# Twenty seeded key shifts after the rounds of a list scheduler, in a two-layer conditioned attention kernel

## The chip, the core and the metric

The kernel runs on one core of one Trainium2 chip. The metric is device microseconds of one execution, taken as the median over runs. The core has a matrix engine (TensorE; PE in the profile, and PEld for its weight loads), three others that compute (VectorE, DVE; ScalarE, ACT; GpSimd, POOL), and SyncE (SP), which here issues nearly all DMAs. Each engine executes its own list of instructions in the order in which the program gives them, and waits on semaphores for the others.

## The reference

Eight sequences of 512 tokens and 512 features pass through two layers, each of which adds its result to its input; all is float32.

```python
# layer 0: linear attention, 8 heads of 64
xn = ln(x)
q = softmax over the head's features of (xn @ Wq + bq)
k = softmax over the tokens of (xn @ Wk + bk + (1 - mask) * -1e6)
v = (xn @ Wv + bv) * mask
y = q @ (k^T v)                       # per head
h = ln(y) * (1 + scale) + shift       # scale, shift = split(silu(emb) @ W_emb + b_emb)
x = x + silu(h) @ W_out + b_out
# layer 1: softmax attention, 16 heads of 32
att = softmax over m of (q_n . k_m + (1 - mask_m) * -1e6)
y = att @ v ; the rest as in layer 0
```

## The kernel before

The kernel writes no engine's list by hand. It records every operation into an object `Order`, then `Order.place` computes a start time and an engine for each operation, and `Order.issue` (the helper on line 483, which is why nearly every row of the profile says L483) emits them sorted by start time. So the order on every engine comes from this planner, which runs on the host before the launch and costs no device time.

**The work.** Layer 0 goes batch by batch: load x, normalise, transpose it on TensorE, project with split weights (a high and a low part of each operand, three products of four matmuls of 512 columns each), softmax, attention, hidden layer, output. Layer 1 works on groups G of four heads (32 groups, four for each batch): `l1_qk` projects, and writes high and low parts `hl` to DRAM (`dWk<-hl`, `dWq<-hl`); `l1_stack` reads them back stacked (`kst<-dWk`, `qst<-dWq`); `l1_max` computes all scores once (`mm<-qst,kst` with 98 rows), takes the row maxima on DVE (`nm<-mm`), transposes them (`mi`), copies them out on ACT (`z<-mm`), and sends them by DMA into rows 98 to 106 of the stack (`qst<-z`); `l1_att` computes the scores a second time with 106 rows, so that the maximum is already subtracted, and ACT takes the exponential (`A<-mm`); `l1_av` multiplies by v in four column groups of 32 (`mm<-A,v`, eight instructions a block) and `A<-A,A` on POOL or DVE sums the exponentials. The last group is done by `l1_last` in halves, and after it come the hidden layer and output of the last batch.

**The planner.** An operation (`Op`) has the engines that may run it with a duration for each (`_takes`), its dependences (`deps`, `soft`), and the tiles that it opens (`fresh`), each of which waits for a free buffer. `pack` is a list scheduler: it keeps a clock for every engine, takes the engine that can start something earliest, and gives it, of the operations that are ready at that time, the one with the smallest `key`; an engine is not kept idle for a more urgent operation that is not ready yet. `slack` then walks backwards from the end and sets each key to the latest start that the operations behind it allow. The first keys are the program's order. A round is one `pack` and one `slack`; `place` does twelve and keeps the placement that ends first. Besides the durations the planner charges TensorE for three things:

```python
if at > now[e] + 1.0:
    o.start += WEIGHTS                      # 110 ns after any wait
elif many != narrow:
    o.start += ENTER if many else LEAVE     # 95, 150 ns around a block in column groups
```

A DMA ends 2400 ns (`DMA_LAND`) after its bytes have passed one common pipe of 260 bytes a ns, and its issue takes 560 ns of its queue.

Of 'A<-A,A' and of a few other operations the planner also chooses the engine (`order.on("gpsimd", "vector")`).

Of the kernel before, what the change touches and what calls it, by code (L numbers as in the profile page):

```python
# [172 lines left out]
class Op:  # L173
    __slots__ = (
        "seq", "engines", "calls", "takes", "late", "deps", "users", "waits", "tiles", "fresh",
        "ready", "start", "end", "engine", "bytes", "key", "soft", "after",
    )


ENTER, LEAVE = 95.0, 150.0  # L180
ROUNDS = 12
LINK = {"PE": 55.0, "ACT": 36.0, "DVE": 36.0, "POOL": 90.0, "SP": 60.0}
WEIGHTS = 110.0
DMA_ISSUE, DMA_LAND, DMA_RATE = 560.0, 2400.0, 260.0
# [2 lines left out]
class Room:  # L187
# [6 lines left out]
    def lets(self, place, taken):  # L194
        free = len(self.free) - taken
        if place == self.head + taken:
            return free > 0
        return self.loose and free > 1

    def take(self, place):  # L200
        self.gone.add(place)
        while self.head in self.gone:
            self.gone.discard(self.head)
            self.head += 1
        return heapq.heappop(self.free)
# [8 lines left out]
class Order:  # L214
# [44 lines left out]
    def add(self, name, calls, takes, late, nbytes=0):  # L259
        if not isinstance(takes, dict):  # L260
            takes = {name: takes}
        o = Op()
        o.seq, o.calls, o.late, o.bytes = len(self.ops), calls, late, nbytes
        o.takes = {ENGINES[k]: (k, v) for k, v in takes.items()}
        o.deps, o.soft, o.users, o.after, o.tiles, o.fresh = set(), set(), [], [], [], []
        o.start = o.end = o.engine = None
        o.key = o.seq
        for t in self.hold:
            self.touch(o, t, None, True)
        self.hold = []  # L270
        for method, args, kw in calls:
            outs, ins = [args[0]], list(args[1:])
            for k, v in kw.items():
                (outs if k == "accum_out" else ins).append(v)
            for v in ins:
                if isinstance(v, View):
                    self.touch(o, v.tile, v.box(), False)
            for v in outs:
                if isinstance(v, View):
                    box = v.box()  # L280
                    if method == "matmul":
                        box = (*box[:2], 0, 511)
                    self.touch(o, v.tile, box, True)
        o.deps.update(self.behind)
        o.soft -= o.deps | {o}
        for d in o.deps:
            d.users.append(o)
        for d in o.soft:
            d.after.append(o)
        self.ops.append(o)  # L290

# [23 lines left out]
        kept.append((o, box, write))  # L315
        t.seen = kept

    def place(self, rounds=ROUNDS):

        best = None  # L320
        for _ in range(rounds):
            end = self.pack()
            if best is None or end < best[0]:
                best = end, [(o.start, o.end, o.engine, [t.slot for t in o.fresh]) for o in self.ops]
            self.slack(end)
        for o, (o.start, o.end, o.engine, slots) in zip(self.ops, best[1]):
            for t, t.slot in zip(o.fresh, slots):
                pass
        return best[0]

    def slack(self, end):

# [1137 lines left out]
```

## Time and profile before

| | |
|---|---|
| median of 3 runs | 1383.26 us (1383.21 to 1383.97) |
| the profiled execution, its own time | 1382.37 us |
| its span, first to last instruction | 1380.3 us |
| instructions | 20884 |
| mean granted TensorE clock | 0.993 |
| DMA | 158.85 MB, mean 115 GB/s |

The profile is of one execution, so a sum made from it stands against 1382.37 us, of which 2.1 us lie outside the span; the median lies 0.9 us above. Layer 0 fills the span to about 527 us, layer 1 the rest. In the views, a time is in microseconds from the start of the span; a busy time of an engine is the union of its instructions, and the matmul's end is modelled, so that PE's busy time includes what lies between the starts of two matmuls as long as the first one's end is later than the second one's start.

### The profile page before, as it was taken

How to read it: one execution, taken by the hardware profiler on the slowest of the kernel's cores; microseconds unless marked ns; L12 is line 12 of the kernel's file. 1: busy time of each engine (PE TensorE's matmuls, PEld its weight loads, DVE VectorE, ACT ScalarE, POOL GpSimd, SP SyncE). 2: the span in 40 equal slices, each digit the busy share in tenths (PEclk: the TensorE clock that was granted, in tenths of full speed). 3: DMA queues.
4: the chain of work that ended last, by engine and by line, in shares of the span. 5: the costliest groups of instructions: out<-in, count | busy, mean ns of one | idle time of the engine just before them, and what ended most of it. 6: DMA issues, size and time to landing. Idle time of an engine off the chain costs nothing.

```text
span 1380.3 us, 20884 instructions
## 1 busy us (share of the span) xinstructions
PE 1345.3 (97%) x7363; PEld 944.0 (68%) x7363; DVE 1034.7 (75%) x1771; ACT 747.8 (54%) x1400; POOL 684.2 (50%) x748
## 2 busy tenths in 40 slices
PE   6999999999999999999999999999999999999987
PEld 4788788888888886566566566566666566666645
DVE  6676576666767777887878787778878867878966
ACT  4433334433345535556847756855855864764773
POOL 6222504133232525676555647548538636655663
PEclk9999999999999999999999999999999999999999
DMA  6332203012221374553263364463563544445312
GB/s 226 132 129 93 98 5 100 32 69 92 69 100 60 112 236 114 142 150 110 94 178 98 94 186 106 116 185 69 153 173 76 151 140 110 140 119 140 95 43 69
DMA packets 77375, 158.85 MB, mean 115 GB/s; under 512 B 8556, under 2 KB 8680, under 8 KB 77248
## 3 DMA queue, kind: packets, MB, share of 16 engines
q1 hardware_dynamic: 77152, 157.41, 38.9%
q8 instruction: 58, 0.95, 0.3%
q14 instruction: 45, 0.37, 0.1%
q0 software_dynamic: 64, 0.08, 0.0%
q10 hardware_dynamic: 56, 0.04, 0.0%
HBM read 104.92 MB, written 50.48 MB: 113 GB/s over the span
## 4 chain that ended last, share of the span: by engine, by line
PE 90%; ACT 3%; DMA 3%; DVE 2%; issue 1%; POOL 1%; SPq 0%; ACTq 0%; POOLq 0%
PE mm L483 90%; DMA qst<-z 2%; ACT mm L483 1%; DMA qst<-dWq 1%; ACT y L483 1%; DVE nm L483 0%; DMA v<-x 0%; DVE xc L483 0%; DMA dWq<-hl 0%; ACT xT L483 0%; DVE A L483 0%; ACT z L483 0%; ACT A L483 0%; DMA v<-in_mask_BxS_ff 0%; DVE xT L483 0%
## 5 line engine op out<-in xcount | busy, mean ns | idle before, releaser
L483 POOL TENSOR_TENSOR A<-A,A 128x512 f32<-128x512 f32 x249 | 332.7, 1358 | 214.1 <-PE mm L483 148.2
L483 DVE TENSOR_REDUCE nm<-mm 128x1 f32<-128x512 f32 x512 | 332.7, 683 | 71.4 <-PE mm L483 68.3
L483 ACT ACTIVATE A<-mm 128x512 f32<-128x512 f32 x450 | 251.1, 602 | 144.3 <-PE mm L483 136.8
L483 PE MATMUL mm<-kst,qst 98*128 98x512 f32 x512 | 202.6, 422 | 4.5 <-DMA qst<-dWq 2.3
L483 PE MATMUL mm<-qst,kst 106*128 106x512 f32 (+1 forms) x528 | 194.6, 409 | 3.6 <-DMA qst<-z 3.4
L483 PEld LDWEIGHTS mm<-kst,qst 98*128 98x128 f32 x512 | 97.0, 192 | 73.0 <-issue 21.4
L483 PE MATMUL mm<-A,v 128*32 128x512 f32 (+1 forms) x932 | 145.4, 593 | 0.0
L483 PEld LDWEIGHTS mm<-qst,kst 106*128 106x128 f32 x528 | 98.7, 192 | 55.8 <-issue 15.8
L483 POOL TENSOR_TENSOR y<-y,bo 128x512 f32<-128x512 f32 x60 | 78.1, 1308 | 101.2 <-DMA y<-in_x 90.8
L483 PE MATMUL mm<-Wvh,xT 128*128 128x512 f32 x384 | 120.2, 402 | 0.0
L483 PE MATMUL mm<-xT,Wkh 128*128 128x512 f32 x384 | 117.4, 413 | 1.2 <-ACT xT L483 0.8
L483 ACT ACTIVATE mm<-mm,cols 128x512 f32<-128x512 f32 x64 | 48.2, 753 | 121.9 <-PE mm L483 121.9
L483 PE MATMUL mm<-ident,xc 128*128 128x128 f32 x512 | 92.5, 284 | 14.9 <-DVE xc L483 12.0
L483 POOL TENSOR_SCALAR v<-bWv,cols 128x512 f32<-128x512 f32 x64 | 48.2, 768 | 115.2 <-PE mm L483 115.2
L483 ACT ACTIVATE y<-mm,shL,scL 128x128 f32<-128x128 f32 (+1 forms) x144 | 76.4, 531 | 51.0 <-PE mm L483 48.5
L483 PEld LDWEIGHTS mm<-ident,xc 128*128 128x128 f32 x512 | 65.1, 144 | 44.4 <-DVE xc L483 13.6
L483 DVE TENSOR_TENSOR A<-A,A 128x512 f32<-128x512 f32 x73 | 83.6, 1155 | 14.9 <-PE mm L483 12.3
L483 PEld LDWEIGHTS mm<-xT,Wkh 128*128 128x128 f32 x384 | 69.8, 191 | 22.3 <-ACT xT L483 6.0
L483 PEld LDWEIGHTS mm<-Wvh,xT 128*128 128x128 f32 x384 | 71.7, 189 | 16.5 <-issue 1.7
L483 ACT ACTIVATE mm<-mm,shL,scL 128x128 f32<-128x128 f32 (+2 forms) x152 | 76.1, 501 | 7.2 <-PE mm L483 7.2
L483 PE MATMUL mm<-xT,Wqh 128*128 128x512 f32 x256 | 76.4, 399 | 0.3 <-DVE nm L483 0.2
L483 POOL MEMSET bWk<- 64x4 f32 (+1 forms) x24 | 5.9, 245 | 136.1 <-PE mm L483 135.4
(204 smaller groups left out, 2704.1 us busy)
## 6 DMA issues: line engine op xcount, KB each, us to landing
kst<-dWk SPq DMA_DIRECT2D x96, 256.0 KB
qst<-dWq SPq DMA_DIRECT2D x96, 256.0 KB
dWk<-hl SPq DMA_DIRECT2D x32, 512.0 KB
dWq<-hl SPq DMA_DIRECT2D x32, 512.0 KB
xc<-in_x SPq DMA_DIRECT2D x32, 256.0 KB
y<-in_x SPq DMA_DIRECT2D x32, 256.0 KB
x<-y SPq DMA_DIRECT2D x32, 256.0 KB
xc<-x SPq DMA_DIRECT2D x32, 256.0 KB
```

What stands on the lines that cost most here:

```text
L483: getattr(engine, method)(*args, **kw)
```

## The change

The planner does eight rounds in place of twelve, and goes on from the keys after the best of them. Twenty times, `moved` draws from a fixed seed a share (1, 3 or 10 per cent) of the operations' groups and a spread (500, 2000 or 6000 ns), and shifts the keys of each drawn group by a Gaussian number; a group is the operations whose first tile has the same name without digits, within 120 operations of the program's order. Two rounds follow from the shifted keys, and the result replaces the best only if it ends earlier by the planner's own clock. At the end the best keys are packed once more. The lists of users, which were filled in the order of a Python set, are now filled in the program's order. No recorded operation, duration, buffer count or constant of the planner's charges is changed.

```diff
+import random
@@ class Op
-        "ready", "start", "end", "engine", "bytes", "key", "soft", "after",
+        "ready", "start", "end", "engine", "bytes", "key", "soft", "after", "group",
-ROUNDS = 12
+ROUNDS = 8
+MOVES = (30003, 30024, 30032, 30040, 30090, 30221, 30224, 30234, 30236, 30247, 30369, 30408, 30455, 30462, 30463, 30480, 30512, 30517, 30536, 30622)
@@ def add
-        for d in o.deps:
+        for d in sorted(o.deps, key=lambda d: d.seq):
             d.users.append(o)
-        for d in o.soft:
+        for d in sorted(o.soft, key=lambda d: d.seq):
             d.after.append(o)
@@
-    def place(self, rounds=ROUNDS):
-
-        best = None
-        for _ in range(rounds):
+    def place(self):
+
+
+        best = self.rounds([o.seq for o in self.ops], ROUNDS)
+        for seed in MOVES:
+            best = min(best, self.rounds(self.moved(best[1], seed), 2), key=lambda r: r[0])
+        self.rounds(best[2], 1)
+        return best[0]
+
+    def rounds(self, line, n):
+        best = (1e12,)
+        for o, key in zip(self.ops, line):
+            o.key = key
+        for _ in range(n):
+            line = [o.key for o in self.ops]
             end = self.pack()
-            if best is None or end < best[0]:
-                best = end, [(o.start, o.end, o.engine, [t.slot for t in o.fresh]) for o in self.ops]
             self.slack(end)
-        for o, (o.start, o.end, o.engine, slots) in zip(self.ops, best[1]):
-            for t, t.slot in zip(o.fresh, slots):
-                pass
-        return best[0]
+            if end < best[0]:
+                best = end, [o.key for o in self.ops], line
+        return best
+
+    def moved(self, line, seed):
+        draw = random.Random(seed)
+        share, size = draw.choice([0.01, 0.03, 0.1]), draw.choice([500.0, 2000.0, 6000.0])
+        shift = {g: draw.gauss(0.0, size) for g in self.groups() if draw.random() < share}
+        return [key + shift.get(o.group, 0.0) for o, key in zip(self.ops, line)]
+
+    def groups(self):
+        for o in self.ops:
+            o.group = re.sub(r"\d", "", o.tiles[0].name), o.seq // 120
+        return sorted({o.group for o in self.ops})
```

## The prediction

> **What bounds the kernel now.** I read the page first, for which engine fills the span:
>
> ```profile
> span 1380.3 us, 20884 instructions
> PE 1345.3 (97%) x7363; PEld 944.0 (68%) x7363; DVE 1034.7 (75%) x1771; ACT 747.8 (54%) x1400; POOL 684.2 (50%) x748
> PE 90%; ACT 3%; DMA 3%; DVE 2%; issue 1%; POOL 1%; SPq 0%; ACTq 0%; POOLq 0%
> ```
>
> TensorE is busy for 1345.3 of 1380.3 us and carries 90% of the chain that ended last. The next engine, DVE, has 345 us to spare. The change adds and removes no matmul, so order can only win back what TensorE loses: 35.0 us of idle time, stretches at a lower clock, and small gaps that the busy time conceals. The busy time by stages tells where the idle part lies (columns: stretch and its length, busy time with instructions of PE, PEld, DVE, ACT, POOL, then granted clock, DMA share, GB/s):
>
> ```profile
> 0.00:18.30 18.30, 4.90 (x18) 3.21 (x18) 10.03 (x19) 5.66 (x9) 11.51 (x30) 1.00 0.84 271
> 18.30:527.00 508.70, 508.34 (x3075) 417.57 (x3076) 351.07 (x699) 207.31 (x368) 167.67 (x258) 1.00 0.29 97
> 527.00:533.00 6.00, 4.06 (x29) 3.32 (x28) 3.75 (x8) 5.91 (x11) 5.38 (x5) 1.00 0.79 222
> 533.00:541.00 8.00, 8.00 (x25) 4.29 (x24) 7.17 (x12) 4.91 (x9) 0.34 (x2) 0.57 0.94 224
> 570.00:1297.00 727.00, 721.43 (x3679) 457.23 (x3678) 577.46 (x917) 456.84 (x873) 434.14 (x399) 1.00 0.46 127
> 1297.00:1377.00 80.00, 70.12 (x397) 41.36 (x395) 59.09 (x86) 50.24 (x104) 42.28 (x39) 0.91 0.27 75
> ```
>
> Idle: 13.4 us in the head, 0.4 in layer 0, 1.9 at the border of the layers, 0.5 between 541 and 570, 5.6 in layer 1, 9.9 in the tail, and 3.3 after TensorE's last matmul. The fourth row's clock of 0.57 over 8 us is 3.4 us lost; the tail's 0.91 over 70 busy us is 6.3 us.
>
> The timeline of PE in layer 1 shows the concealed gaps (start, length, instruction):
>
> ```profile
> 614.96 0.40 PE L483 MATMUL mm<-kst,qst 98*128 98x512 f32 x1
> 615.19 0.39 PE L483 MATMUL mm<-Wvl,xT 128*128 128x512 f32 x1
> 615.51 1.06 PE L483 MATMUL mm<-A,eg 128*32 128x512 f32 x8
> 616.39 1.04 PE L483 MATMUL mm<-A,v 128*32 128x512 f32 x8
> 617.37 0.73 PE L483 MATMUL mm<-Wvl,xT 128*128 128x512 f32 x2
> ...
> 619.93 0.48 PE L483 MATMUL mm<-Wvh,xT 128*128 128x512 f32 x1
> 620.25 0.39 PE L483 MATMUL mm<-kst,qst 98*128 98x512 f32 x1
> ```
>
> Matmuls of 512 columns start 0.23 to 0.24 us apart. Into the block in column groups it takes 0.32, so 0.09 more. Two blocks behind one another are 0.88 apart, and out of the second it takes 0.98, so 0.10 more: a block that stands alone costs 0.19 us beyond its work. From 619.93 to 620.25 a lone step takes 0.32, again 0.09 more: a weight load that came late because it waited. None of this is idle time. The planner charges 95, 150 and 110 ns for these three, so it sees what the chip pays, a little dear. Its durations also stand near the rows: by its formula 685 ns for `nm<-mm` (the groups show 683), 598 for `A<-mm` on ACT (602), 1408 for `A<-A,A` on POOL (1358). I take from this that most of an earlier end by its clock should be an earlier end on the chip.
>
> **The change, by stages.** By its own clock the search can't end later than its first eight rounds; the first eight may end later than the best of twelve, and what the shifts find is not in any row. So I bound each stage by what TensorE loses there and by what the rule of `pack` lets a key change.
>
> *Head* (13.4 us idle). The chain shows DVE's `xc` waiting for POOL's `rsf`, which stands behind the mask's work. But the `mvf` that POOL's next step needs is done at 7.1 us, POOL's `hl` from 6.81 to 8.07 was already running, and `pack` never holds an engine idle. What a key can change is `mbd<-hl` (8.37 to 8.95) ahead of `vef` (9.03): 0 to 0.7 us. I take 0.5.
>
> *Layer 0* (0.4 us idle in 508.7): TensorE is full. I take 0, with 2 us either way for the small gaps.
>
> *Border of the layers.* TensorE idles 1.94 us before 532.80, waiting for the last parts of `xT`. The chain there is ACT's:
>
> ```profile
> 527.91 0.62 ACT Woh L483
> 528.52 0.66 ACT mm L483
> ...
> 529.69 0.57 ACT z L483
> ```
>
> `Woh` is the cast of a weight whose partner is finished at 533 us and later; with another key it stands behind `mm`, and 0.62 us, with `z` 1.2 us, leave the chain. If the gap goes, the 3.4 us at the lower clock behind it may go too: 0 to 5.3 us. I take the middle, 2.7. What is late next is DMA `qst<-z`, issued at 530.28, whose reader starts at 534.80, behind a wait of 0.64 us of the weight load.
>
> [...]
>
> *Layer 1, 570 to 1297.* Idle 5.6 us. The waits of weight loads, from 600 to 1297 (us in total, times, longest):
>
> ```profile
> PEld mm L483 <- issue: 78.9, 175, 0.8
> PEld mm L483 <- ACT A L483: 29.6, 63, 0.9
> ```
>
> With the smaller rows of the same answer these are some 360 waits; at 0.09 us, 32 us. The blocks are 31 groups of heads by four, 124; at 0.19, 24 us. Together with the idle time 61 us are at stake, but each block stands where its exponentials are ready, and the rate is even (509 matmuls from 600 to 700, 508 from 800 to 900), so I count on one part in fifteen: 4 us. Bounds: 12 us gained (a fifth), 6 lost (a tenth, if the shifted order meets more waits than the planner believes).
>
> *Tail* (1297 to the end, 83.3 us). Idle 9.9 and 6.3 at the lower clock. The chain:
>
> ```profile
> 1305.31 8.34 DMA qst<-dWq
> 1329.19 3.09 DMA qst<-z
> 1349.64 4.61 DMA v<-x
> ```
>
> The three reads `qst<-dWq` are issued behind three `kst<-dWk`, `kst<-mbd` and a `y<-x` on SP; the `v<-x` delays only POOL's `v` ahead of `veb` and `rsb`. Both are matters of order, and here a few places decide the end directly. Bounds: 15 us gained, 3 lost. I take a third, 5. The last 3.3 us, one DVE addition and its store, stay.
>
> Sum: 0.5 + 0 + 2.7 + 4 + 5 = 12.2 us. 1382.4 - 12.2 = 1370.2 for the profiled execution; the median lies 0.9 higher, 1371.
>
> **The rivals.**
>
> *The maxima's round trip falls due (slower).* In each of 32 groups, `nm`, `mi`, `z` and the DMA `qst<-z` must be through before `mm<-qst,kst`. The trace shows the DMA at 3.1 to 4.2 us in the chain, TensorE idle for it 3.4 us in six places and weight loads 1.8 in five. The planner prices it at 3.5 us from issue and knows no contention; shifts that pull the second scores up to that price make the shortfall of 0.7 (4.2 - 3.5) due at all 32: 22 us against 12 gained, 1393. It decides once more than half of the groups wait. Against it: twenty shifts that touch at most a tenth of the groups hardly reach all 32. Chance 0.11.
>
> *The chip does not follow, or the shifts find little (no change).* If eight rounds end about as late as twelve and few shifts lower the end, or what they save is lost to waits that the planner misses: within 2.8 us of 1383.3. For it: TensorE is full in 92% of the span. Chance 0.10.
>
> *The gain is near the bounds.* Border 5, layer 1 10, tail 10, head 0.7: 26 us, 1357. For it: the clock returns with the gaps, which the planner doesn't even count. Against it: it needs three stages at once. Chance 0.14.
>
> **How the numbers follow.** The forecast, 1371 with 1361 to 1380 of its own, has 0.65. Faster by over 0.2% (2.8 us, about what a measurement of this kernel can tell from no change) is 0.65 + 0.14 = 0.79, no change 0.10, slower 0.11. The range leaves out most of the slower rival and the lower half of the large gain: 1357 to 1384.
>
> **What the profile would show.** The same 7363 matmuls, PE busy near 1339 us and idle time near 29 (about half of the 12 us is idle time, by the shares above). Right: a tail from the last `dWq<-hl` on shorter by some 5 us, with PE's clock above 0.91; no stretch at 0.57 behind the border, or a shorter one; fewer than 360 waits of weight loads in layer 1. The split of `A<-A,A` between POOL and DVE may shift without meaning. Wrong: PE idle before `mm<-qst,kst` on `qst<-z` above 15 us (the slower rival); or the stages as long as before to 1 us each (the second); or a gain that lies in layer 0, which I hold to be full.

## The result and the profile after

The changed kernel takes 1387.89 us (median of 7 runs, 1386.20 to 1393.48) against 1383.21 us before (7 runs): ratio 1.0041, 95% interval 1.0026 to 1.0055. It is slower by 0.4%, where 1371 us was forecast. The profiled execution has a span of 1384.4 us, 4.1 us more than before.

The page of the changed kernel:

```profile
span 1384.4 us, 20891 instructions
...
PE 1343.9 (97%) x7363; PEld 940.1 (68%) x7363; DVE 1043.3 (75%) x1776; ACT 746.6 (54%) x1400; POOL 681.0 (49%) x743
...
PE 91%; DVE 4%; ACT 2%; DMA 2%; issue 1%; POOL 0%; SPq 0%; ACTq 0%; DVEq 0%
```

The work is the same: 7363 matmuls, and five sums have gone from POOL to DVE (1771 to 1776, 748 to 743). But TensorE is idle for 40.5 us instead of 35.0, and DVE's part of the chain has doubled to 4%. The busy time by the stages of the prediction:

```profile
18.30:527.00 508.70, 508.70 (x3072) 415.91 (x3073) 350.05 (x699) 207.26 (x369) 165.30 (x257) 1.00 0.29 97
527.00:533.00 6.00, 5.58 (x35) 4.15 (x34) 5.72 (x9) 5.63 (x10) 4.94 (x5) 1.00 0.93 232
533.00:541.00 8.00, 8.00 (x39) 5.50 (x38) 7.16 (x12) 5.47 (x10) 1.59 (x3) 1.00 0.92 237
541.00:570.00 29.00, 27.57 (x137) 15.52 (x135) 25.29 (x37) 16.62 (x31) 22.74 (x17) 0.94 0.38 109
570.00:1297.00 727.00, 715.10 (x3640) 450.86 (x3640) 579.66 (x909) 451.30 (x859) 427.06 (x391) 1.00 0.45 126
```

At the border the gap of 1.94 us and the stretch at a lower clock are gone (from 533 to 541 the clock is 1.00 with 39 matmuls, where it was 0.57 with 25), though a smaller gap has opened behind them (28.5 to 27.6 busy us, clock 0.94). Layer 1 has lost: 715.1 busy us and 3640 matmuls in the same 727 us, against 721.4 and 3679. Most of it lies in one place. The same 40 us of both kernels, the kernel before first, the changed one second:

```profile
1140.00:1180.00 40.00, 40.00 (x218) 25.22 (x218) 32.90 (x56) 20.80 (x41) 30.27 (x29) 1.00 0.37 90
```

```profile
1140.00:1180.00 40.00, 36.51 (x189) 23.02 (x188) 32.62 (x50) 16.41 (x30) 23.13 (x21) 0.96 0.39 100
```

Twenty-nine matmuls fewer. The timeline of the changed kernel there (start, length, instruction, and in brackets the idle time before it and what ended it):

```profile
1152.04 1.29 POOL L504 TENSOR_TENSOR A<-A,A 128x512 f32<-128x512 f32 x1
...
1153.28 1.29 POOL L504 TENSOR_TENSOR A<-A,bWq 128x512 f32<-128x512 f32 x1
1153.50 6.01 DVE L504 CAST mi<-nm 128x16 fp32r<-128x16 f32 x1
...
1154.52 2.52 POOL L504 TENSOR_TENSOR A<-A,A 128x512 f32<-128x512 f32 x2
...
1157.00 1.27 POOL L504 TENSOR_TENSOR A<-A,bWk 128x512 f32<-128x512 f32 x1
...
1158.22 1.27 POOL L504 TENSOR_TENSOR A<-A,A 128x512 f32<-128x512 f32 x1
...
1159.55 0.17 DVE L504 TENSOR_TENSOR mi<-nm,mi 128x16 fp32r<-128x16 f32 x1
...
1159.87 1.01 PE L504 MATMUL mm<-ident,mi 128*8 128x128 f32 x4 [3.49 <-DVE mi L504]
```

A cast of 16 elements a partition, which elsewhere lasts as little as 0.17 us, lasts 6.01 us. It ends as POOL's run of sums ends (1158.22 + 1.27 = 1159.49, against 1153.50 + 6.01 = 1159.51); each of the sums starts before the one ahead of it has ended. The profile counts the cast as busy time of DVE, so it is part of DVE's total (1034.7 us before, 1043.3 now) and of no wait. TensorE runs out of work and idles 3.49 us, and from 1159.4 its clock is 0.51 for 3.4 us.

**Where the plan and the chip part.** `place` gives each instruction of TensorE a planned start, and the trace holds the same instructions in the same order, so the two can be laid side by side. The table takes the transposes of the maxima (`mm<-ident,mi`) of some of the 32 groups as marks. Columns two and three are the kernel before; the others are differences from it, of the planned start (P) and of the start in the trace (T).

| mark | before P | before T | change P | change T | change, DVE relieved T |
|---|---|---|---|---|---|
| group 0 (layer 0 ends) | 524.6 | 529.0 | -3.0 | 0.0 | +0.6 |
| group 1 (border) | 545.5 | 550.3 | -3.6 | -1.1 | -0.8 |
| group 23 | 1118.2 | 1127.3 | -6.8 | +2.3 | -0.8 |
| group 25 | 1168.7 | 1178.7 | -6.8 | +7.4 | -0.7 |
| group 30 (tail begins) | 1288.1 | 1298.1 | -8.2 | +6.5 | -1.6 |
| end | 1367.1 | 1380.3 | -8.5 | +4.1 | -4.1 |

By its own clock the change ends 8.5 us earlier. On the chip it is level through layer 0, gains 1.1 us at the border, loses 3.4 up to group 23 and 5.1 from there to group 25, and takes back 0.9 up to group 30 and 2.4 in the tail. The last column is an experiment below, with the same planned starts.

Each T column is one execution. What happens between groups 23 and 25 repeats in the runs below: the three traces of the changed order with the stall (`pair_after`, the changed kernel again, and `after_mi` among them) take 56.4 to 56.5 us from mark to mark, the two with DVE relieved 51.4 and 51.5, and the five with the order before 51.4 to 51.5. The ends repeat less well. A second trace of the kernel before (`pair_before`) ends 5.1 us after the first, and a second trace with DVE relieved (`pair_after_lopool`) ends 1.1 us ahead of it, not 4.1.

Eight rounds in place of twelve, and the ordered lists, do nothing: without any shift the new planner gives every operation the planned start and engine that it has in the kernel before. The twenty shifts are the whole change.

### The profile page after: what moved, and what is told of

The parts are those of the page before. It is cut to its first block, busy times and chain, and to the rows that moved or that the text cites. A ratio compares the mean times of both kernels' runs of the same rounds, so it can differ in the third digit from the quotient of the medians.

```text
span 1384.4 us, 20891 instructions
## 1 busy us (share of the span) xinstructions
PE 1343.9 (97%) x7363; PEld 940.1 (68%) x7363; DVE 1043.3 (75%) x1776; ACT 746.6 (54%) x1400; POOL 681.0 (49%) x743
## 4 chain that ended last, share of the span: by engine, by line
PE 91%; DVE 4%; ACT 2%; DMA 2%; issue 1%; POOL 0%; SPq 0%; ACTq 0%; DVEq 0%
PE mm L504 91%; DVE nm L504 1%; ACT mm L504 1%; DVE A L504 1%; DVE mi L504 1%; ACT y L504 1%; DMA qst<-z 1%; DVE xc L504 0%; POOL A L504 0%; DMA rawL0Wk<-in_L_cond_Wk 0%; DMA out<-y 0%; DVE y L504 0%; DMA v<-in_mask_BxS_ff 0%; ACT A L504 0%; DVE stf L504 0%
## 5 line engine op out<-in xcount | busy, mean ns | idle before, releaser
L504 POOL TENSOR_TENSOR A<-A,A 128x512 f32<-128x512 f32 x243 | 329.2, 1376 | 212.4 <-PE mm L504 126.2
L504 PE MATMUL mm<-A,v 128*32 128x512 f32 (+1 forms) x932 | 141.7, 586 | 0.3 <-ACT A L504 0.2
L504 PE MATMUL mm<-Wvh,xT 128*128 128x512 f32 x384 | 125.2, 407 | 0.0
L504 PE MATMUL mm<-xT,Wkh 128*128 128x512 f32 x384 | 121.1, 415 | 1.9 <-ACT xT L504 1.4
L504 PE MATMUL mm<-ident,xc 128*128 128x128 f32 x512 | 101.6, 286 | 16.6 <-DVE xc L504 12.5
L504 DVE TENSOR_TENSOR A<-A,A 128x512 f32<-128x512 f32 x79 | 89.1, 1135 | 14.9 <-PE mm L504 10.4
L504 ACT ACTIVATE hl<-mm,cols 128x512 fp32r<-128x512 f32 x64 | 44.2, 691 | 54.5 <-PE mm L504 47.8
```

What stands on the lines that cost most here:

```text
L504: getattr(engine, method)(*args, **kw)
```

## The experiments

Medians of the kernel before differ from set to set (1381.5, 1390.3, 1382.6 and 1384.2 us in the four sets below, the last two on one chip), so kernels are compared within a set; a ratio is to the kernel before in the same set.

**First set: the cast, and part of the shifts.** `after_mi` and `before_mi` issue the cast as a reduction; the plan stays the same to the nanosecond.

```diff
-        nc.vector.tensor_copy(mi[:, :, 0, :], nm)
+        nc.vector.tensor_reduce(mi[:, :, 0, :], nm.unsqueeze(3), AX.X, ALU.max)
```

> The changed kernel with the same placement; only the first of the two small instructions on the maxima (the cast mi<-nm, 128x16, SBUF to SBUF, on DVE) is issued as a reduction over an axis of length one, with the same result. Theory 'held cast': in the trace of the changed kernel one cast lasts 6.01 us, as long as POOL runs sums back to back, and TensorE then idles 3.5 us and has half the clock for 3.4 us; if a reduction is not held, this costs nothing, and the kernel falls by about 5 us to 1382 to 1384, no cast above 0.3 us. Rival 'spread loss': the search's gains are lost in many small pieces, and the one stall only stands for time that would be lost elsewhere: 1386 to 1389.

Measured: 1386.5 us, ratio 1.0028 (1.0005 to 1.0051). The reduction is not held (0.15 to 0.17 us in all 32 groups), but the next DVE instruction is, at the same place and to the end of the same run of sums (1152.96 + 5.86 = 1158.82, against 1157.53 + 1.26 = 1158.79; timeline of `after_mi`):

```profile
1152.58 1.28 POOL L504 TENSOR_TENSOR A<-A,bWq 128x512 f32<-128x512 f32 x1
1152.75 0.17 DVE L504 TENSOR_REDUCE mi<-nm 128x16 fp32r<-128x16 f32 x1
...
1152.96 5.86 DVE L504 TENSOR_TENSOR mi<-nm,mi 128x16 fp32r<-128x16 f32 x1
...
1153.83 2.52 POOL L504 TENSOR_TENSOR A<-A,A 128x512 f32<-128x512 f32 x2
...
1156.31 1.25 POOL L504 TENSOR_TENSOR A<-A,bWk 128x512 f32<-128x512 f32 x1
...
1157.53 1.26 POOL L504 TENSOR_TENSOR A<-A,A 128x512 f32<-128x512 f32 x1
...
1158.96 0.60 PE L504 MATMUL mm<-ident,mi 128*8 128x128 f32 x4 [3.34 <-DVE mi L504]
```

So the experiment did not take the stall away (TensorE still idles 3.34 us) and decided nothing on its cost. It shows what is held: not every DVE instruction at this point, for the reduction ran through while POOL was busy, though its operands lie in SBUF as well; held were the cast and the subtraction.

> The kernel before, placement unchanged, with the same replacement of the cast by a reduction. 'Held cast': its casts last 0.56 us in the median and 2.4 at most, nearly all hidden behind TensorE's other work, so 0 to 2 us faster (1381 to 1383). 'Spread loss': the same as before, 1383. If it falls by 5 us or more, the cast's delay is a cost of both kernels alike and no reason for their difference.

Measured: 1380.3 us, ratio 0.9997 (0.9972 to 1.0023): no change, as both theories had it.

The first five and the first ten shifts alone:

```diff
-MOVES = (30003, ..., 30622)
+MOVES = (30003, 30024, 30032, 30040, 30090)
```

> The changed planner with the first five of the twenty shifts: by the planner's clock 3.0 us earlier than the kernel before. 'Held cast': 1380 to 1383, as long as no cast above 3 us appears in its trace. 'Spread loss': within 1 us of 1383 or above it, with the lateness against the planner's clock 3 us larger than before's.

> The first ten of the twenty shifts: by the planner's clock 5.7 us earlier than the kernel before. 'Held cast': 1378 to 1382 unless a cast above 3 us appears. 'Spread loss': 1383 to 1387, rising with the number of shifts.

Measured: 1387.6 us (1.0028, 1.0004 to 1.0052) and 1385.6 us (1.0029, 1.0002 to 1.0056). Neither has a cast above 1.31 us, so "held cast", which had both at 1383 us or below, fails on both. The timeline of `moves5` has another DVE instruction held, a sum, behind three of POOL's and into the instructions that follow:

```profile
607.26 3.78 POOL L504 TENSOR_TENSOR A<-A,A 128x512 f32<-128x512 f32 x3
...
607.55 4.04 DVE L504 TENSOR_TENSOR A<-A,bWq 128x512 f32<-128x512 f32 x1
```

That explains at most 3.4 us of it (4.04 less the 0.68 of the shortest sum `A<-A,A` of this shape on DVE in the trace of before). The time does not rise with the number of shifts either, against "spread loss"; the planned gain of 3.0 and 5.7 us simply does not appear.

**Second set: DVE relieved, and controls without a gain.** In `after_lopool` and `before_lopool` the subtraction is issued on POOL as well, at its place in the planned order; planned starts are unchanged.

```diff
+                    if method == "tensor_tensor" and o.tiles[-1].tag == "mi":
+                        nc.gpsimd.tensor_tensor(*args, **kw)
+                        continue
                     getattr(engine, method)(*args, **kw)
```

> The changed kernel, placement unchanged; the cast of the maxima is issued as a reduction, and the subtraction that follows it (mi<-nm,mi, which lasted 5.86 us at the same place when only the cast was replaced) is issued on POOL, at its place in the planned order, so that DVE holds neither up nor is held. Theory 'held instruction': the stall near 1154 us is a DVE instruction that waits as long as POOL runs sums back to back; now both small instructions together take under 2 us everywhere, TensorE's idle 3.3 to 3.5 us there is gone with the half clock behind it, and the kernel falls by 4 to 6 us, to about the kernel before's time. Rival 'spread loss': the stall goes and the time does not, ratio to before above 1.002.

> The kernel before, placement unchanged, with the same two replacements. It has no stall of this kind in its trace (longest cast 2.4 us), so both theories have it within 0.2% of the kernel before; POOL's 0.35 us a group may cost up to 2 us.

Measured: 1378.9 us (6 runs, 1378.0 to 1380.3; ratio 0.9922, 0.9903 to 0.9941) and 1380.1 us (7 runs; 0.9939, 0.9917 to 0.9961). The first speaks against "spread loss", which had a ratio above 1.002, but lies further down than "held instruction" had it, at about the time of the kernel before. The second fails both theories: they had it within 0.2% of the kernel before, or up to 2 us slower, and it is 0.6% faster. The kernel before was at 1390.3 us on this chip, with a mean granted clock of 0.989 to 0.991 in 20 of its 24 runs, where all runs of the two relieved kernels but one have 0.993 or more; why, no run shows. So the two are better compared with each other (1.2 us apart, within their intervals), and the fourth set repeats them. The timeline of `after_lopool` at the place of the stall:

```profile
1150.41 0.17 DVE L507 TENSOR_REDUCE mi<-nm 128x16 fp32r<-128x16 f32 x1
...
1151.38 1.28 POOL L507 TENSOR_TENSOR A<-A,A 128x512 f32<-128x512 f32 x1
...
1152.45 0.74 DVE L507 SCALAR_TENSOR_TENSOR v<-mm,cols,v 128x512 f32<-128x512 f32 x1
...
1152.63 0.21 POOL L505 TENSOR_TENSOR mi<-nm,mi 128x16 fp32r<-128x16 f32 x1
```

The subtraction waits in POOL's own line for the sum that is running, then takes 0.21 us, and the same stretch of 40 us is full again (busy time by stretches, `after_lopool`):

```profile
1140.00:1180.00 40.00, 39.87 (x217) 24.59 (x215) 29.64 (x54) 21.09 (x40) 30.79 (x30) 1.00 0.35 86
```

The controls replace the rule that keeps a move only if the plan ends earlier:

```diff
-            best = min(best, self.rounds(self.moved(best[1], seed), 2), key=lambda r: r[0])
+            best = self.rounds(self.moved(best[1], seed), 2)
```

> A control: twelve shifts of the same kind, each followed by two rounds and taken whether it gains or not, chosen so that the planner's clock stays within 0.5 us of the kernel before's (1367.4 against 1367.1 us). It moves TensorE's order as far as the changed kernel does (60% of the steps at the old place against 51%, mean displacement 1.7 places in both). Theory 'lucky draw': orders within 1% of one another by the planner's clock are not ranked by it, the kernel before's order is one that happens to suit the chip, and any reshuffle loses: 1384 to 1390. Rival 'squeeze': it is the search that picks orders whose waits the planner misses, so a reshuffle without a gain costs nothing: 1380 to 1383.

> A second control of the same kind from other seeds (planner's clock 1367.4; 57% of the steps at the old place, mean displacement 1.8). 'Lucky draw': 1384 to 1390. 'Squeeze': 1380 to 1383. If the two controls differ by more than 4 us, the spread between orders of equal plan is itself larger than what the search plans to win.

Measured: 1385.8 us both (0.9971, 0.9953 to 0.9989; and 0.9971, 0.9958 to 0.9984), 6 to 7 us above the two relieved kernels of the same set. Since the kernel before stood at 1390 there, they do not tell whether a reshuffle loses against its usual 1383. `neutral1` shows the hold again, in an order that won nothing by plan: the cast lasts 7.19 us at 1258.95, and TensorE is busy for 14.93 of the 20 us around it (timeline, then busy time by stretches).

```profile
1258.95 7.19 DVE L504 CAST mi<-nm 128x16 fp32r<-128x16 f32 x1
```

```profile
1255.00:1275.00 20.00, 14.93 (x65) 8.97 (x62) 16.90 (x19) 5.00 (x9) 13.75 (x13) 0.83 0.32 73
```

**Third set: two other searches, and a third control, on one chip.** `climb1` and `climb2` differ from the change in the seeds alone.

> The changed planner with twenty other kept shifts, found in the same way from other seeds; by the planner's clock 1359.9 us, 7.3 earlier than the kernel before. 'Lucky draw': the search's gain is real on average and a reshuffle's loss is on top, so 1378 to 1386, below the controls' mean. 'Squeeze': slower than the kernel before and than the controls, 1384 to 1390.

> Another twenty kept shifts; by the planner's clock 1360.2 us, 6.9 earlier than the kernel before. 'Lucky draw': 1378 to 1386. 'Squeeze': 1384 to 1390.

> A third control, twelve shifts without a gain (planner's clock 1367.15; 64% of the steps at the old place, mean displacement 1.4). 'Lucky draw': 1384 to 1390. 'Squeeze': 1380 to 1383.

Measured: 1385.1 us (1.0025, 1.0009 to 1.0040), 1380.4 us (0.9992, 0.9981 to 1.0003) and 1382.7 us (1.0003, 0.9992 to 1.0014). The two searches plan 7.3 and 6.9 us and lie 2.4 above and 2.3 below a control that plans nothing and is level with the kernel before. "Lucky draw" fails on the control, "squeeze" on `climb2`. What stands is that two orders 7 us ahead by plan came out within 3 us of one that plans nothing, and on either side of it. The hold does not sort these three: the longest cast is 2.42 us in the trace of `climb1`, 1.26 in `climb2`, and 4.40 in `neutral3`, which is level with the kernel before all the same. Why `climb1` won nothing stays open.

**Fourth set: the four corners on one chip.**

> The changed kernel once more, unaltered, on one chip with the next three. 'Held instruction': 1384 to 1390, with a DVE instruction on the maxima of 5 us or more near 1154 us in its profile. 'Spread loss': 1384 to 1390 as well, whether or not such an instruction shows.

> The changed kernel with the two small instructions of the maxima taken off DVE's contended path (cast as a reduction, subtraction on POOL). 'Held instruction': 1377 to 1381, 5 us or more below the changed kernel on the same chip. 'Spread loss': within 2 us of the changed kernel.

> The kernel before with the same two replacements. If what is left of the search's gain without the held instruction is real, this is 1 to 5 us slower than the changed kernel with the replacements; if nothing is left of it, the two agree to 1 us.

> The kernel before, unaltered, as a profiled run. 'Held instruction': if its time on this chip is near 1381, its profile has no DVE instruction on the maxima above 3 us; if its time is near 1390, as on one of the chips, the profile has one or more, so that the hold is what separates its runs. 'Spread loss': no relation.

| | DVE as it was | DVE relieved |
|---|---|---|
| order before | 1382.6 us (0.9977, 0.9959 to 0.9995) | 1382.8 us (0.9970, 0.9949 to 0.9991) |
| order of the change | 1388.4 us (1.0027, 1.0003 to 1.0050) | 1380.1 us (0.9962, 0.9945 to 0.9980) |

Twelve runs each; the ratios are to 35 runs of the kernel before (median 1384.2). The top left corner is that same kernel, and its interval leaves out 1, so a difference of 0.2% means little here. The relief is worth nothing in the order before (0.2 us the other way) and 8.3 us in the order of the change, where the two sets of twelve do not overlap (1377.3 to 1383.9 against 1384.8 to 1395.0). With it the changed order is 2.7 us ahead; without it 5.8 behind. The hold repeats in this profile of the change (6.06 us; the cast's shortest, median and longest):

```profile
L504 DVE CAST mi<-nm x32: 168/654/6062, 526.1 to 1327.9; 128x16 fp32r<-128x16 f32 x32
```

The last expectation failed: this time the profile of the kernel before fell on a run of 1387.5 us, and its longest cast is 1.15 us. So the hold separates the two orders, and it is not what separates the kernel before's own runs (1379.1 to 1387.5 here). Those go in part with the clock: of the 35 runs, the four at 0.995 or above took 1379.0 to 1381.1 us, the nine at 0.991 or below 1386.6 to 1395.6. The trace of `pair_before` shows one such place, 1.6 us of its 5.1. These are the same steps of the two traces of the kernel before, 2 us apart, with 0.28 and 0.29 us of idle time in 8 us (the first trace, then `pair_before`):

```profile
788.00:796.00 8.00, 7.72 (x36) 5.09 (x36) 5.35 (x7) 5.18 (x10) 3.35 (x3) 1.00 0.16 66
```

```profile
790.00:798.00 8.00, 7.71 (x26) 5.82 (x26) 4.09 (x5) 3.92 (x8) 2.96 (x2) 0.79 0.02 6
```

What brings the lower clock on in one run and not in another stays open.

The changed order with DVE relieved is the fastest kernel of each of its two sets: 0.9962 and 0.9922 of the kernel before, in the second set by no more than the noise.

## Why the prediction was wrong

*The reading of the bound* held. TensorE fills the span, the same matmuls run, and the loss shows as TensorE's idle time.

*Head, 0.5 forecast.* Nothing came: the first projection (`mm<-xT,Wkh`) starts at 18.30 us, where it stood at 18.31.

*Layer 0, 0 taken.* Right, and it hides the first part of the planned gain. The plan of before lets TensorE wait seven times in layer 0, 5.0 us in all, for the high part of the hidden layer; in the trace the same seven steps come 0.7 us late. The search cut the planned waits there to 2.7 us, and the chip had nothing to give: 3.0 us earlier by plan, 0.0 by the trace. The two other searches repeat it (1.8 and 2.3 planned, 1.5 and 0.4 us later in the traces).

*Border, 2.7 forecast.* It gave 1.1 (1.1 to 1.4 in the five traces of the changed order, relieved or not). The gap and the lower clock behind it (0.51 from 534.0 to 540.8) went together, as forecast, but the wait that I had named as next in line came due: TensorE now idles 1.43 us before `mm<-qst,kst` at 554.56 on the DMA `qst<-z`, and from 555.2 its clock is 0.51 for 3.4 us. That the clock falls with the gap, on which 1.7 us of this term rested, did not hold each time: from 541 to 570 TensorE idles 1.43 us in all in the changed kernel, at a mean clock of 0.94, and 1.64 us in `pair_after`, where the clock stays at 1.00.

*Layer 1, 4 forecast, bounds 12 gained and 6 lost.* This is the step that failed. By plan the stage does gain 4.6 us (from 3.6 ahead to 8.2); on the chip it lost 7.6 (from 1.1 ahead to 6.5 behind), outside my bounds. I had costed it in waits of weight loads, with every duration a constant. From 600 to 1297 there are 363 of these waits in both kernels, not fewer, so that part gave nothing either way. What I had put at nothing is the spread of a duration. I compared the planner's prices with mean durations and found them close; the planner gives both instructions on the maxima 900 ns, and the means, 0.65 and 1.01 us, fit. The spread was in the trace of before, and I did not look at it (shortest, median and longest, in ns):

```profile
L483 DVE CAST mi<-nm x32: 174/562/2409, 526.9 to 1324.3; 128x16 fp32r<-128x16 f32 x32
```

The order of the change puts one cast beside a run of five sums that leave no gap on POOL, and the cast lasts until the last of them ends (1159.51 against 1159.49). The four corners price the holds on the two instructions together: 8.3 us on the medians, of which the traces show 5.1 at the place itself. Most of the rest may lie between groups 1 and 23, where the three traces of the changed order without full relief lose 2.6 to 3.4 us and the two with it 0.0 and 0.6; but the five traces with the order before spread over 2.5 us there, so this part is not shown.

Why the cast and the subtraction are held there and a reduction is not (0.17 us at the same place in `after_mi`), no run shows. Nor does one show why the hold lasts over several of POOL's sums of 1.3 us and not over one: the holds of 6.01 and 5.86 us cover five of them, and that of 7.19 us in `neutral1` six.

*Tail, 5 forecast.* It gave 2.4 (82.2 to 79.8 us from the last but one mark to the end); but the traces differ among themselves as much, 78.6 to 83.4 us with the order before and 79.7 to 81.4 with the changed one, relieved or not, so this gain is not clear of the noise.

*The rivals.* The slower one named the right chain (`nm`, `mi`, `z`, `qst<-z`) and the wrong link: TensorE's idle time on `qst<-z` is as before (3.4 to 3.3 us), and no shortfall spread over 32 groups; one group lost most of it, on DVE. My argument against that rival was weak as well: each shift touches at most a tenth of the groups of operations, but after all twenty only 51% of TensorE's steps stand at their old place. The second rival, that the chip does not follow the planner, is what the other searches show: 7.3 and 6.9 us planned, and neither clearly ahead. In the change itself, without the hold, 2.7 us is left of the 8.5 planned, about what a measurement of this kernel can tell from no change. I gave it 0.10, and took closeness of prices for closeness of plans; a plan that is 13 us short of the chip before cannot be trusted to rank orders 8 us apart.

## What to carry to other kernels

A search over orders improves what its cost model prices, and moves cost into what it does not price: before trusting a planned gain, compare it with the span by which plan and chip already differ, and with the span by which two runs of one kernel differ, and look at the longest duration of an instruction, not only at its mean. A small instruction on a critical chain whose duration varies by a factor of ten may be waiting for something, even if the profile calls it busy; here the cast took 0.17 to 6.01 us, and the longest ended 0.02 us after POOL's run of sums. Move such an instruction to a form or an engine where its longest duration is short (here a reduction, 0.15 to 0.17 us, and POOL, 0.21 to 0.73), and only then compare orders.

## What the runs showed of the hardware that was not expected

On DVE the cast `mi<-nm` (6.01 us in the changed kernel, 7.19 in `neutral1`) and the subtraction `mi<-nm,mi` (5.86 in `after_mi`) lasted to the end of a whole run of POOL's back-to-back sums of 1.3 us, within 0.03 us, and not only to the end of the one that was running; a reduction during the same run took 0.17 us (`after_mi`). Most delays are shorter: the 73 sums `A<-A,A` of 128x512 on DVE last 0.68 to 1.84 us in the trace of before, so none is longer than the shortest by more than 1.16 us, less than one such sum takes on POOL (1.36 us in the mean). What makes a delay long or short was not settled. And a clock of 0.51 came for 6.8 us after an idle gap of 1.94 us in the order before, and for 3.4 us after gaps of 1.43 and 3.49 us in the changed one, while 1.64 us of idle time between 541 and 570 left the clock at 1.00 (`pair_after`), and the clock was 0.79 over 8 us with 0.29 us of idle time (`pair_before`). The amount of idle time alone does not decide it.
